# The input side of twelve pairs of steps of a GRU, computed beside the first steps, and other chunk sizes

## The chip, the cores and the metric

The kernel runs on one core of a Trainium2 chip. Its engines work side by side, each in the order of its own program: TensorE (PE; PEld is its loading of weights), VectorE (DVE), ScalarE (ACT), GpSimd (POOL) and SyncE (SP, which here issues DMA transfers). The metric is the device time of one execution in microseconds, as the median of several runs. A profile is one execution of its own.

## The reference

A GRU with 16 sequences (B), 256 steps (T) and 512 features (D) runs over x, from the state `cond_2048`. Its states go through a layer of 8 experts of rank 128, of which each token takes the two likeliest, and the result is added to x.

```python
def cell(h, x):
    gi = x @ W_ih + b_ih
    gh = h @ W_hh + b_hh
    i_r, i_z, i_n = jnp.split(gi, 3, axis=-1)
    h_r, h_z, h_n = jnp.split(gh, 3, axis=-1)
    r = jax.nn.sigmoid(i_r + h_r)
    z = jax.nn.sigmoid(i_z + h_z)
    n = jnp.tanh(i_n + r * h_n)
    h_new = (1.0 - z) * n + z * h
    return (h_new, h_new)
...
router_logits = x / norm @ router_w
routing_weights = jax.nn.softmax(router_logits.astype(jnp.float32), axis=-1)
rw, selected_experts = jax.lax.top_k(routing_weights, TOP_K)
rw = rw / jnp.sum(rw, axis=-1, keepdims=True)
...
for e in range(N_EXPERTS):
    out = out + combine[:, e, None] * (x @ Wa[e] @ Wb[e])
...
x = x + _L0_ffn_ref(_L0_cond_ref(cond_2048, x, ...), ...)
```

All of it is in 32-bit floats.

## The kernel before

**The recurrence.** The 256 steps are 32 blocks of 8 (`TS`), and 128 pairs `m` of two steps. The gates of a step stand in two PSUM banks, `rn` (r, the hidden part of n, the input part of n) and `z`; there are two sets of banks, one for even pairs and one for odd. For a pair, `seed` (L250) copies the biases into its banks with ScalarE, `trans_x` (L260) turns a tile of x with VectorE, and `gate_in` (L268) adds the input's product with `W_ih` on PE, a quarter `q` of the features at a time: 4 matmuls into `rn` (L273) and 4 into `z` (L281). Each 32-bit matmul stands as two records in the profile. The two quarters of one step belong to the next pair. `step` (L826) adds the state's product with `W_hh` (L837, L847), and then ScalarE and VectorE compute r (L863), z (L868), n (L870 to L872) and the new state (L875 to L879), which is turned into `hist` (L882) for the next step's matmuls. `back` (L887) turns it back as `h` (L890).

**The experts.** The first 29 blocks go a sparse way, in four chunks of `CHUNKS` blocks. After a block, its `Route` writes the states to DRAM (L520, eight transfers), computes the router's logits (L345) and the top two. After a chunk, a `Chunk` ranks the tokens (L372, L377), reads the states back (L468, tiles `ht2`) and scatters them by expert into slots in DRAM (L474, issued by GpSimd). A `Slab` is 128 slots of one expert: its rows are loaded (L575), GpSimd copies the expert's weights (L593, L597), VectorE turns the rows (L603), PE multiplies down (L614) and up (L629), ScalarE copies the result (L621, L637), and SP stores it (L638). A `Combine` gathers both results of each token (L666), loads x (L662), adds (L680) and stores a block of the output (L684). The last three blocks, 29 to 31, take a dense way, `Moe`: all experts (L749, L770, L786), with stores at L797.

**The planner.** The order of all this work around the steps is made in Python, when the program is built. Each agent (`Route`, `Chunk`, `Slab`, `Combine`, `Moe`) has a plan of pieces; a piece has a cost in microseconds of PE, the least number of steps since the piece before (`gap`), PE's work, what the other engines do then, and which rooms it takes and gives (`ROOM`, counts of buffers). In every step `choose` (L967) goes through the agents by rank and picks pieces. A slab's or a dense block's piece may be picked up to 0.5 us in a step, and beyond it where a running `credit`, fed from the work left and the steps left to its due time, allows. The PE part stands behind the step's own matmuls and `gate_in`, the rest behind `back`. After the last step the loop goes on until no agent is left; what it picks then makes up the tail. `keep_order` (L33) fixes the order on each engine as it was written out.

Before the first step stand the loads of all weights, in SP's queue. `clear` (L209) puts zeros into the slots, one transfer a step from step 6 on. `load_x` (L122) brings x for the block after next, in the fourth step of a block.

Of the kernel before, what the change touches and what calls it, by code (L numbers as in the profile page):

```python
# [20 lines left out]

P = 128
TS = 8
CHUNKS = [6, 10, 8, 5]
LAG = 10

ROOM = {
    "ps": 3, "xg": 4, "wg": 4, "xt": 2, "at": 2, "yg": 2, "xr": 3, "a": 1, "aT": 1,
    "hc": 2, "load": 2, "copy": 1, "turn": 2,
}  # L30


# [10 lines left out]
def gru_moe_kernel(  # L43
# [10 lines left out]
    wb: bass.AP,  # L54
    out: bass.AP,
):

# [184 lines left out]


    xts = {}

    seeds = []

    def seed(m):  # L250

        if m < T // 2:
            for n, b in enumerate((bias[:, 0:3, :], bias[:, 3:4, :])):
                b = b.rearrange("p g d -> p (g d)")
                ins = act.copy(banks[m % 2][n][:, 0 : b.shape[1]], b).ins
                if seeds:
                    tc.add_manual_dep(ins, seeds[-1].name, SYNC, reason="seen")
                seeds.append(ins)

    def trans_x(m):  # L260
        if m < T // 2:
            xt = xtp.tile([P, NQ, 32], FP, tag="xT", name=f"xT_{m}")
            dve.transpose(
                xt.rearrange("p q c -> p (q c)"), xs[m // NM][:, m % NM, :]
            )
            xts[m] = xt

    def gate_in(m, q, seen=None):  # L268

        w = wih[:, q, :].rearrange("p (g j d) -> p g j d", g=3, j=NJ)  # L270
        rn, zb = banks[m % 2]
        for j in range(NJ):
            pe.matmul(  # L273
                rn[32 * j : 32 * j + 32, 0 : 3 * P].rearrange(
                    "p (g d) -> p g d", g=3
                )[:, 0:3:2, :],
                lhsT=xts[m][:, q, :], rhs=w[:, 0:3:2, j, :],
                start=False, stop=(q == NQ - 1), skip_group_check=True,
            )
        for j in range(NJ):  # L280
            ins = pe.matmul(  # L281
                zb[32 * j : 32 * j + 32, 0:P],
                lhsT=xts[m][:, q, :], rhs=w[:, 1, j, :],
                start=False, stop=(q == NQ - 1), skip_group_check=True,
            ).ins
            if seen is not None and j == 0:
                tc.add_manual_dep(ins, seen.name, SYNC, reason="seen")
# [53 lines left out]
    def router(h):  # L341

        for q in range(NQ):
            for c in range(NJ):
                pe.matmul(  # L345
                    rt[32 * c : 32 * c + E, 0:32].rearrange("p (b t) -> p b t", t=TS),
                    lhsT=wr_sb[:, q, :], rhs=tokens(h, q, c),
                    start=(q == 0), stop=(q == NQ - 1),
                )


    class Chunk:
# [111 lines left out]
            self.w = [whi, wlo]  # L464

        def fetch(self, k):
            ht = moe.tile([P, D], FP, tag="ht2", bufs=3, name=f"ht2_{self.c}_{k}")
            sp.dma_start(ht, self.rows[k].rearrange("b t d -> (b t) d"))  # L468
            self.ht = getattr(self, "ht", {})
            self.ht[k] = ht  # L470
# [21 lines left out]
        def plan(self):  # L492
            k = self.k
            pieces = [
                Piece(gap=7, cost=0.9, pe=[("ranks",)],
                      then=[("places",), ("places2",)]),
                Piece(then=[("places3",)]),
                Piece(then=[("experts",)]),
                Piece(then=[("weights",)]),
            ] + [Piece() for _ in range(k - 2)]  # L500
            pieces[0].then[:0] = [("fetch", m) for m in range(3)]
            for m in range(k):
                pieces[2 + m].then.append(("scatter", m))
                if m + 3 < k:
                    pieces[2 + m].then.append(("fetch", m + 3))
            return pieces

    class Route:
# [185 lines left out]
    class Moe:  # L694
# [3 lines left out]

        def prep(self):
            i = self.i  # L700
            self.hc = moe.tile([P, NQ, P], FP, tag="hc", name=f"hc_{i}")
            for q in range(NQ):
                pool.tensor_copy(
                    self.hc[:, q, :].rearrange("p (b t) -> p b t", t=TS),
                    self.hist[:, :, q, 16:32].rearrange("p t b -> p b t"),
                )
            self.sq = moe.tile([P, NQ, P], FP, tag="a", bufs=1, name=f"sq_{i}")
            pool.tensor_mul(self.sq, self.hc, self.hc)
# [220 lines left out]
    def at_step(n, make):  # L929
        starts.setdefault(n, []).append(make)  # L930
# [12 lines left out]
    def slabs(c):  # L943
        ch = chunks[c]
        by = ready[c + 1] + 5 if c + 1 < len(CHUNKS) else T + 2
        ch.left = n_slabs[c]
        for n in range(n_slabs[c]):
            begin(Slab(ch, n), 1 + c, by)
# [9 lines left out]
    for c, k in enumerate(CHUNKS):  # L958
        at_step(ends[c] - k * TS, lambda c=c, k=k: chunks.append(Chunk(c, k)))
        at_step(ready[c], lambda c=c: slabs(c))  # L960
    for n in range(2):
        for k in range(n_slots[n]):
            at_step(6 + k + n * n_slots[0], lambda n=n, k=k: clear(n, k))

    credit = 0.0

    def choose():  # L967

        nonlocal credit
        rates = {}  # L970
        for a in agents:
            if a.by is not None:
                rates[a.by] = rates.get(a.by, 0.0) + sum(p.cost for p in a.todo)
        credit += sum(r / max(1, by - now) for by, r in rates.items())
        credit = min(credit, 1.3) if now <= T else 3.5
        spent = 0.0
        picked = []
        stuck = set()
        for a in agents:
            gap = now - a.since  # L980
            while a.todo and a.todo[0].gap <= gap:
                p = a.todo[0]
                key = (a.place, len(a.todo)) if a.place else None
                if key in stuck or any(room[x] < 1 for x in p.takes):
                    break
                if p.cost and a.by is not None:
                    if spent + p.cost > 0.5 and credit < 0.5 * p.cost:
                        break
                    credit -= p.cost
                spent += p.cost  # L990
                for x in p.takes:
                    room[x] -= 1
                picked.append((a, p))
                a.todo.pop(0)
                a.since = now
                gap = 0
            if a.todo and a.place:
                stuck.add((a.place, len(a.todo)))
        return picked
# [25 lines left out]
    for i in range(NB):  # L1025
        rows, rows_next = rows_next, None
        for t in range(TS):
# [8 lines left out]
            elif m + 1 < T // 2:  # L1036
                q = 0 if t % 2 == 0 else 2
                gate_in(m + 1, q)
                gate_in(m + 1, q + 1, seen)
            picked = choose()  # L1040
            advance(0, picked)
            hrow = back(hT, f"h_{i}_{t}")
            advance(1, picked)
# [16 lines left out]
    while agents or starts:  # L1060
        for make in starts.pop(now, []):
            make()
        now += 1
        picked = choose()
        advance(0, picked)
        advance(1, picked)
    keep_order(tc)
# [42 lines left out]
```

## Time and profile before

| | |
|---|---|
| median of three runs | 1322.7 us (1321.27 to 1323.1) |
| the profiled execution | 1321.0 us on the device, span 1319.1 us |
| PE busy | 1255.1 us, 95% of the span |
| VectorE, ScalarE, GpSimd busy | 742.3, 385.0, 269.0 us |
| chain that ended last, by engine | PE 82%, DVE 8%, DMA 5% |
| r (L863), first and last | 37.5 and 1224.1 us |

The page of the profile gives the busy time of each engine, and the costliest groups: L837 with 491.9 us, L273 with 318.7, L847 with 270.1, L281 with 208.5. Matmuls are pipelined, so these overlap, and their sum is no time. A granted clock of 1.0 stands in all slices but the first and the last. In the order of time a line has its start and length in us, the engine, the line of the kernel, the operation, what it writes from what it reads, and in brackets how long the engine was idle before it and what ended that. SPq is SP issuing a transfer, not the transfer itself.

### The profile page before, as it was taken

How to read it: one execution, taken by the hardware profiler on the slowest of the kernel's cores; microseconds unless marked ns; L12 is line 12 of the kernel's file. 1: busy time of each engine (PE TensorE's matmuls, PEld its weight loads, DVE VectorE, ACT ScalarE, POOL GpSimd, SP SyncE). 2: the span in 40 equal slices, each digit the busy share in tenths (PEclk: the TensorE clock that was granted, in tenths of full speed). 3: DMA queues.
4: the chain of work that ended last, by engine and by line, in shares of the span. 5: the costliest groups of instructions: out<-in, count | busy, mean ns of one | idle time of the engine just before them, and what ended most of it. 6: DMA issues, size and time to landing. Idle time of an engine off the chain costs nothing.

```text
span 1319.1 us, 68240 instructions
## 1 busy us (share of the span) xinstructions
PE 1255.1 (95%) x30378; PEld 892.0 (68%) x30378; DVE 742.3 (56%) x2678; ACT 385.0 (29%) x1330; POOL 269.0 (20%) x465
## 2 busy tenths in 40 slices
PE   6899999999999999999999999999999999999993
PEld 3566666666777777777766777777776777777551
DVE  1455555565655555555655766555655656765543
ACT  1222222222323233332332333333233333332220
POOL 2000000021100000000332321111332323543633
PEclk7999999999999999999999999999999999999997
DMA  8622222243221111111444453222543555643786
GB/s 195 178 90 91 90 68 74 87 145 96 67 59 51 46 58 43 59 55 40 162 148 123 140 154 89 71 70 71 162 148 102 148 154 160 195 158 104 220 249 182
DMA packets 142948, 151.58 MB, mean 115 GB/s; under 512 B 20726, under 2 KB 100150, under 8 KB 142652
## 3 DMA queue, kind: packets, MB, share of 16 engines
q1 hardware_dynamic: 133232, 116.74, 30.0%
q0 software_dynamic: 9280, 30.42, 7.3%
q8 instruction: 238, 3.90, 1.2%
q14 instruction: 58, 0.48, 0.1%
q10 hardware_dynamic: 140, 0.05, 0.0%
HBM read 80.28 MB, written 66.85 MB: 112 GB/s over the span
## 4 chain that ended last, share of the span: by engine, by line
PE 82%; DVE 8%; DMA 5%; ACT 2%; SPq 1%; issue 1%; DVEq 0%; ACTq 0%
PE rn L837 35%; PE z L847 17%; PE rn L273 12%; PE z L281 6%; PE at_ps L614 5%; PE y_ps L629 5%; DVE hist L882 2%; DVE zh L875 2%; DVE rows L879 2%; ACT z L868 2%; DVE m L877 2%; DMA whh<-in_L_cond_W_hh_dram 1%; PE rt L345 1%; PE o_ps L786 1%; DMA xg<-x_slots 1%
## 5 line engine op out<-in xcount | busy, mean ns | idle before, releaser
L837 PE MATMUL rn<-whh,hist 128*32 128x256 f32 x8160 | 491.9, 381 | 27.5 <-DVE hist L882 27.2
L837 PEld LDWEIGHTS rn<-whh,hist 128*32 128x32 f32 x8160 | 250.0, 110 | 202.3 <-DVE hist L882 61.4
L273 PE MATMUL rn<-wih,xT 128*32 128x256 f32 x4096 | 318.7, 382 | 8.5 <-DMA wih<-in_L_cond_W_ih_dram 7.2
L870 DVE SCALAR_TENSOR_TENSOR n<-r,rn 128x128 f32<-128x128 f32 x256 | 73.7, 288 | 368.8 <-ACT r L863 368.5
L847 PE MATMUL z<-whh,hist 128*32 128x128 f32 x8160 | 270.1, 273 | 0.0
L847 PEld LDWEIGHTS z<-whh,hist 128*32 128x32 f32 x8160 | 234.5, 110 | 42.8
L281 PE MATMUL z<-wih,xT 128*32 128x128 f32 x4096 | 208.5, 274 | 0.0
L863 ACT ACTIVATE r<-rn 128x128 f32<-128x128 f32 x256 | 71.1, 278 | 433.8 <-PE rn L837 433.6
L281 PEld LDWEIGHTS z<-wih,xT 128*32 128x32 f32 x4096 | 136.2, 111 | 87.7 <-issue 2.4
L273 PEld LDWEIGHTS rn<-wih,xT 128*32 128x32 f32 x4096 | 124.1, 111 | 9.9 <-issue 5.7
L545 POOL TENSOR_TENSOR nrm<-ss,half 128x1 f32<-128x1 f32 x29 | 16.2, 558 | 525.3 <-ACT ht L543 505.1
L875 DVE SCALAR_TENSOR_TENSOR zh<-z,h 128x128 f32<-128x128 f32 x255 | 79.8, 313 | 66.1 <-ACT z L868 65.7
L868 ACT ACTIVATE z<-z 128x128 f32<-128x128 f32 x256 | 71.1, 278 | 151.7 <-PE z L847 151.7
L614 PE MATMUL at_ps<-xgT,wag 128*32 128x128 f32 x2752 | 97.4, 273 | 3.1 <-DVE xgT L603 3.0
L629 PE MATMUL y_ps<-wbg,at 128*32 128x256 f32 x1376 | 95.1, 380 | 0.6 <-ACT at L621 0.6
L637 ACT COPY y<-y_ps 128x512 f32<-128x512 f32 x86 | 50.3, 584 | 125.5 <-PE y_ps L629 109.0
L614 PEld LDWEIGHTS at_ps<-xgT,wag 128*32 128x32 f32 x2752 | 78.8, 110 | 10.9 <-issue 4.4
L882 DVE STREAM_TRANSPOSE hist<-rows 128x128 f32<-128x128 f32 x256 | 79.7, 311 | 8.7
L890 DVE STREAM_TRANSPOSE h<-hist 128x128 f32<-128x128 f32 x256 | 79.7, 311 | 8.7
L879 DVE SCALAR_TENSOR_TENSOR rows<-zh,m 128x128 f32<-128x128 f32 x256 | 76.0, 297 | 8.9
L877 DVE SCALAR_TENSOR_TENSOR m<-z,n 128x128 f32<-128x128 f32 x256 | 79.8, 312 | 0.7 <-ACT n L872 0.7
L597 POOL COPY wbg<-wb_sb 128x512 f32 x86 | 57.7, 671 | 108.4 <-PE y_ps L629 108.3
(124 smaller groups left out, 959.2 us busy)
## 6 DMA issues: line engine op xcount, KB each, us to landing
xg<-x_slots SPq DMA_DIRECT2D x344, 64.0 KB
y_slots<-y SPq DMA_DIRECT2D x86, 256.0 KB
ht<-H SPq DMA_DIRECT2D x58, 256.0 KB
x_slots<-zero SPq DMA_DIRECT2D x50, 256.0 KB
x<-in_x_dram SPq DMA_DIRECT2D x256, 32.0 KB
xr<-in_x_dram SPq DMA_DIRECT2D x32, 256.0 KB
out_dram<-xr SPq DMA_DIRECT2D x32, 256.0 KB
H<-rows SPq DMA_DIRECT2D x232, 32.0 KB
```

Of the source, the lines that this page charges most:

```text
L273: pe.matmul(rn[32 * j : 32 * j + 32, 0 : 3 * P].rearrange("p (g d) -> p g d", g=3)[:, 0:3:2, :], lhsT=xts[m][:, q, :], rhs=w[:, 0:3:2, j, ...
L281: ins = pe.matmul(zb[32 * j : 32 * j + 32, 0:P], lhsT=xts[m][:, q, :], rhs=w[:, 1, j, :], start=False, stop=(q == NQ - 1), skip_group_chec ...
L614: pe.matmul(self.ps[c32, 0:P], lhsT=self.wa[:, q, c32], rhs=self.xt[:, q, :], start=(q == 0), stop=(q == NQ - 1),)
L629: pe.matmul(self.ps[c32, half], lhsT=self.at[:, c32], rhs=self.wb[:, half], start=True, stop=True,)
L837: pe.matmul(rn[32 * j : 32 * j + 32, 0 : 2 * P].rearrange("p (g d) -> p g d", g=2), lhsT=hT[:, q, :], rhs=w(q, j)[:, 0:3:2, :], start=Fals ...
L847: pe.matmul(zb[32 * j : 32 * j + 32, 0:P], lhsT=hT[:, q, :], rhs=w(q, j)[:, 1, :], start=False, stop=(q == NQ - 1), skip_group_check=True,)
L868: seen = act.activation(z, zb[:, 0:P], AF.Tanh, scale=0.5).ins
L875: dve.scalar_tensor_tensor(zh, z, 1.0, hrow, ALU.add, ALU.mult)
L877: dve.scalar_tensor_tensor(m, z, 1.0, n, ALU.subtract, ALU.mult)
L879: dve.scalar_tensor_tensor(hn, zh, 0.5, m, ALU.mult, ALU.subtract)
L882: dve.transpose(hist[:, t, :, lo : lo + 32], hn.rearrange("p (q c) -> p q c", q=NQ))
L890: dve.transpose(hrow.rearrange("p (q c) -> p q c", q=NQ), hT)
```

## The change

Twelve pairs, every fourth from 82 to 126, get their input side another way. An agent `Early` of rank 20 loads the pair's two steps of x with eight transfers, turns them with VectorE, multiplies them with `W_ih` into a PSUM tile of its own, copies it out with ScalarE, lets GpSimd add the biases, and stores the result in DRAM. Sixteen steps before the pair, `back` reads it into a tile `gl`, and `seed` copies that, and not the biases, into the pair's banks. `trans_x` and `gate_in` do nothing for these pairs. In the two steps in which `gate_in` for such a pair would stand, `choose` gets 1.8 us in place of 0.5, and after the last step 0. An `Early` piece is picked only within that bound. The tiles of `Early` share buffers with those of `Slab` and `Combine` (tags `yg0`, `yg1`, `at`). `hc` of the dense blocks has one buffer in place of two, `ht2` two in place of three. The chunks are of 7, 11, 7 and 4 blocks, where they were 6, 10, 8 and 5; the slabs are 21, 29, 21 and 15, where they were 19, 27, 23 and 17: 86 both times.

```diff
-CHUNKS = [6, 10, 8, 5]
+CHUNKS = [7, 11, 7, 4]
+EARLY = list(range(82, 128, 4))
-    "hc": 2, "load": 2, "copy": 1, "turn": 2,
+    "hc": 1, "load": 2, "copy": 1, "turn": 2, "early": 2,
...
     def seed(m):
         if m < T // 2:
-            for n, b in enumerate((bias[:, 0:3, :], bias[:, 3:4, :])):
+            src = early.pop(m) if m in EARLY else bias
+            for n, b in enumerate((src[:, 0:3, :], src[:, 3:4, :])):
...
     def trans_x(m):
-        if m < T // 2:
+        if m < T // 2 and m not in EARLY:
...
     def gate_in(m, q, seen=None):
+        if m in EARLY:
+            return
...
+    class Early:
+        def load(self):
+            m = self.m
+            self.x = slb.tile([P, D], FP, tag="yg1", bufs=2, name=f"xe_{m}")
+            for j in range(NJ):
+                for s in range(2):
+                    p0 = 32 * j + 16 * s
+                    sp.dma_start(
+                        self.x[p0 : p0 + B, 0:P],
+                        x[:, 2 * m + s, j * P : (j + 1) * P],
+                    )
+        def turn(self):
+            self.xt = slb.tile([P, NQ, 32], FP, tag="at", bufs=2, name=f"xTe_{self.m}")
+            dve.transpose(self.xt.rearrange("p q c -> p (q c)"), self.x[:, 0:P])
+        def into(self, what, q):
+            if what == "rn" and q == 0:
+                self.ps = big(f"gi_{self.m}").rearrange("p (g d) -> p g d", g=4)
+            w = wih[:, q, :].rearrange("p (g j d) -> p g j d", g=3, j=NJ)
+            for j in range(NJ):
+                g = self.ps[32 * j : 32 * j + 32]
+                if what == "rn":
+                    pe.matmul(
+                        g[:, 0:3:2, :], lhsT=self.xt[:, q, :], rhs=w[:, 0:3:2, j, :],
+                        start=(q == 0), stop=(q == NQ - 1),
+                    )
+                else:
+                    pe.matmul(
+                        g[:, 3, :], lhsT=self.xt[:, q, :], rhs=w[:, 1, j, :],
+                        start=(q == 0), stop=(q == NQ - 1),
+                    )
+        def keep(self):
+            gi = slb.tile([P, 4, P], FP, tag="yg0", bufs=2, name=f"ge_{self.m}")
+            act.copy(gi[:, 0, :], self.ps[:, 0, :])
+            act.copy(gi[:, 2:4, :], self.ps[:, 2:4, :])
+            pool.tensor_copy(gi[:, 1, :], bias[:, 1, :])
+            pool.tensor_add(gi[:, 0, :], gi[:, 0, :], bias[:, 0, :])
+            pool.tensor_add(gi[:, 2:4, :], gi[:, 2:4, :], bias[:, 2:4, :])
+            self.gi = gi
+        def store(self):
+            self.dram = dramc.tile([P, 4, P], FP, name=f"gd_{self.m}")
+            sp.dma_start(self.dram, self.gi)
+            at_step(2 * self.m - 16, self.back)
+        def back(self):
+            early[self.m] = moe.tile([P, 4, P], FP, tag="gl", name=f"gl_{self.m}")
+            sp.dma_start(early[self.m], self.dram)
+        def plan(self):
+            pieces = [
+                Piece(then=[("load",)], takes="early"),
+                Piece(gap=2, then=[("turn",)], takes="at"),
+            ] + [
+                Piece(gap=0, cost=c, pe=[("into", what, q)])
+                for what, c in (("rn", 0.43), ("z", 0.22))
+                for q in range(NQ)
+            ] + [Piece(then=[("store",)], gives="early")]
+            pieces[2].gap, pieces[2].takes = 1, ["ps"]
+            pieces[9].then, pieces[9].gives = [("keep",)], ["ps", "at"]
+            return pieces
...
-            ht = moe.tile([P, D], FP, tag="ht2", bufs=3, name=f"ht2_{self.c}_{k}")
+            ht = moe.tile([P, D], FP, tag="ht2", bufs=2, name=f"ht2_{self.c}_{k}")
...
-            pieces[0].then[:0] = [("fetch", m) for m in range(3)]
+            pieces[0].then[:0] = [("fetch", m) for m in range(2)]
             for m in range(k):
                 pieces[2 + m].then.append(("scatter", m))
-                if m + 3 < k:
-                    pieces[2 + m].then.append(("fetch", m + 3))
+                if m + 2 < k:
+                    pieces[2 + m].then.append(("fetch", m + 2))
...
-            self.hc = moe.tile([P, NQ, P], FP, tag="hc", name=f"hc_{i}")
+            self.hc = moe.tile([P, NQ, P], FP, tag="hc", bufs=1, name=f"hc_{i}")
...
+    at_step(2, lambda: [begin(Early(m), 20) for m in EARLY])
...
-    def choose():
+    def choose(spare):
...
-                    if spent + p.cost > 0.5 and credit < 0.5 * p.cost:
+                    if spent + p.cost > spare and credit < 0.5 * p.cost:
                         break
                     credit -= p.cost
+                if isinstance(a, Early) and spent + p.cost > spare:
+                    break
...
-            picked = choose()
+            picked = choose(1.8 if m + 1 in EARLY else 0.5)
...
-        picked = choose()
+        picked = choose(0.0)
```

More of the change, by code (lines that the diff above doesn't have):

```diff
@@ L246, in gru_moe_kernel @@
     xts = {}
+    early = {}
     seeds = []
@@ L349, in router, with __init__ @@
                 )
+    class Early:
+        def __init__(self, m):
+            self.m = m
+        def load(self):
[54 more added lines that the diff above has]
+            return pieces
```

## The prediction

> **What bounds the kernel now.** I looked first at busy time by stretches of 50 us, because one core that is 95% busy on average can still be bound by two different things. The columns are the stretch, then for PE, PEld, DVE, ACT and POOL the busy us with the count of instructions, then clock, DMA share and GB/s.
>
> ```profile
> 200.00:250.00 50.00, 47.03 (x1143) 32.71 (x1138) 27.00 (x111) 13.77 (x52) 1.08 (x6) 1.00 0.20 64
> 400.00:450.00 50.00, 50.00 (x1256) 35.79 (x1249) 27.93 (x109) 16.27 (x59) 3.78 (x9) 1.00 0.17 48
> 1100.00:1150.00 50.00, 50.00 (x1280) 38.16 (x1272) 33.85 (x115) 16.52 (x55) 18.46 (x26) 1.00 0.60 176
> ```
>
> PE seems full from 400 us on, yet that says nothing of pace: the starts of r (L863) are 4.40 us apart at 200 us and also at 400 us, and about 5.2 us apart at 1100 us. So I went to the order of time on PE within a step, first at 200 us (start, length, line):
>
> ```profile
> 201.65 0.61 PE L273 MATMUL rn<-wih,xT 128*32 128x256 f32 x8
> 202.08 0.40 PE L281 MATMUL z<-wih,xT 128*32 128x128 f32 x8
> 202.78 0.42 PE L837 MATMUL rn<-whh,hist 128*32 128x256 f32 x4 [0.30 <-DVE hist L882]
> ```
>
> The input side of one quarter takes 0.43 us of issue for r and n (201.65 to 202.08) and 0.22 for z, so 0.65, and 1.30 us in a step. After it PE waits for the new state. By issue the hole is 202.78 - 202.30 = 0.48 us. At 400 us one slab piece of 0.43 us fills it and the step stays at 4.40. The step is then bound by the loop of the recurrence: 1.9 us of L837, the two tanh, five VectorE operations. Late, the hole is overfilled:
>
> ```profile
> 1104.84 1.05 PE L629 MATMUL y_ps<-wbg,at 128*32 128x256 f32 x16
> 1105.70 0.63 PE L614 MATMUL at_ps<-xgT,wag 128*32 128x128 f32 x16
> 1106.14 1.92 PE L837 MATMUL rn<-whh,hist 128*32 128x256 f32 x32
> ```
>
> Three pieces (1.29 us by issue) lie between 1104.84 and 1106.14 and L837 has no wait any more: PE sets the end. From the starts of r, grouped by the pieces that stand in the built order of PE, the medians are 4.40 us with 0 or 1 piece, 4.77 with 2, 5.20 with 3, 5.63 with 4. This gives the rule I sum by: **step = the larger of 4.405 and 3.91 + X**, with X the extra PE work (3.91 = 4.77 - 0.86). Over steps 2 to 255 it gives 1170.3 us; measured are 1182.3. The 12.0 us between are ranks, late transfers and the collision shown below.
>
> After the last step (its r at 1224.12) come 95 us of tail: PE works until 1298.4, and then 20.7 us pass on SP's queue alone:
>
> ```profile
> 1299.17 0.58 SPq L797 DMA_DIRECT2D out_dram<-xr  x1
> 1299.83 0.56 SPq L684 DMA_DIRECT2D out_dram<-xr  x1
> 1300.48 2.15 SPq L662 DMA_DIRECT2D xr<-in_x_dram  x2
> 1305.69 3.18 SPq L684 DMA_DIRECT2D out_dram<-xr  x2
> 1308.96 0.59 SPq L662 DMA_DIRECT2D xr<-in_x_dram  x1
> 1314.50 0.55 SPq L684 DMA_DIRECT2D out_dram<-xr  x1
> ```
>
> Block 31's store (L797) waits for the last matmul. Behind it in SP's order stand three loads of xr, with their adds and stores.
>
> **The change, part by part.** 1. *Late steps.* In 24 steps (the two before each of the 12 pairs, steps 163 and 164 to 251 and 252) 1.30 us of L273 and L281 are gone, so there the rule is 2.61 + X, and the planner may put 1.8 us there. 24 x 1.30 = 31.2 us are moved. I put the built PE order of both programs through the rule, step by step. Before: 46 steps with two pieces lose 0.37 each (16.8), 25 with three lose 0.79 (19.9), 19 others, mostly with a route, 14.8: 51.5 us over the floor. After: 23 lose 0.37 (8.4), 19 lose 0.79 (15.1), 14 others 12.3: 35.8 us. **-15.7 us**. Not all 31 come back. Chunk 1's slabs may begin 17 steps later (step 165, not 148), so about a dozen steps there that carried two or three pieces now carry one. Two of the freed steps fill partly with the last pair's own pieces, and steps 221 and 222 stand empty.
>
> 2. *Early steps.* 11 pairs run in steps 6 to 85, the twelfth at 163 to 169. A step takes either 0.43 or 0.44 us, which fits 0.48: no price on PE, as at 400 us. Without this cover (where ranks fall together with a piece) it would be 0.4 us each. ACT gets two copies per pair (0.27 as L621 has, about 0.38 between L255's 0.27 and 0.49), before the seed; the seed ends 2.4 us before the next r in the timeline, so they fit.
>
> 3. *The turn on VectorE.* 12 more transposes (0.28, L263's row) stand behind h (L890) in the order; from there to the next n VectorE has some 2.4 us free. What queues behind a late turn is n (L870), and with it the whole loop. Each waits for 8 loads issued two steps (8.8 us) earlier. SP needs 3.6 to 4.8 us for eight loads of x, 8.8 to 9.7 us for eight stores of H. The worst case is a load placed right behind the stores (step 41): 1.7 + 9.7 + 4.2 us of issue and about 2.2 to land make 17.8 after step 40's r; the cover ends at 17.9. The first two pairs queue 16 loads behind the 2 MB of wb_sb, which hold SP to 1.07 us per load until 55.5 us; landing 58 to 62 against a cover to 59.7. I take +2, from 0 to +6.
> [...] The rows above, with eight in flight and two steps of cover, give +2.
>
> 4. *GpSimd's adds.* 36 operations (0.43 as L703; adds between 0.43 and 1.03 by L703 and L708). The trace has such a meeting:
>
> ```profile
> 311.93 0.72 POOL L597 COPY wbg<-wb_sb 128x512 f32 x1
> 312.09 0.70 DVE L877 SCALAR_TENSOR_TENSOR m<-z,n 128x128 f32<-128x128 f32 x1
> ```
>
> L877 takes 0.28 elsewhere, and this step took 4.82, 0.42 more. 36 meetings would be 15 us; but beside 172 copies of weights only 15 of 254 steps exceed the rule by over 0.15 us with no rank in them. I take +1.5, from 0 to +5.
> [...]
>
> 5. *ht2 with two buffers, not three.* A block's scatter holds GpSimd 2.3 us, and landing plus refetch some 5 more (one fetch shows 4.09 in the chain of waits), so two buffers give a block every 3.7 us against a step of 4.4. POOL's own waits for ht total 6.2 us now. +2, from 0 to +6.
> The 12 stores and 12 reloads (0.4 us of SP each) have 13 steps until the seed that needs them; I take nothing; a reload that misses its seed would stop ACT, and r behind it, for its landing, 2 to 4 us.
>
> 6. *Tail.* Until block 30's last matmul PE has 51.4 us of work now and takes 57.2 from the last r; after, 50.7 us, but the 13 slabs left stand denser (3.4 us each, not 4.1), against SP's 2.0 us of xg loads, y store and combine per slab. I take 59.3, **+2**, from -2 to +8. With hc single, block 31 starts behind block 30: route, 64 matmuls (7.08), two turns, 64 matmuls (7.07), as now 17.1 less one y piece (0.86): 16.3 us. Its xr waits for the second combine's store, lands some 18.1 later; add 0.7, three adds more 2.3, last store 4.6 to the end: 25.7 us after block 30's end. Now it is 1319.1 - 1281.3 = 37.8, since three loads queue behind L797; in the new order none does, and the last chunk has four blocks. **-12**, from -14 to -3.
>
> **Sum** against the profiled span: -15.7 + 2 + 1.5 + 2 + 2 - 12 = -20.2, so 1319.1 to 1298.9. That run took 1321.0 on the device, 1.7 under the median of the three (1322.7); 1322.7 - 20.2 is about **1302 us**.
>
> **The rivals.** *A: filled on paper only.* PE's order is known, its waits are not. In a freed step an "up" needs ACT's copy and a y buffer of two; in the tail ACT's y copies waited 16.5 us for y stores. If the dense steps and slabs lose a third of the two gains: +9, about 1311. Against it: only 5 us of the tail's 57 are PE waits today.
> *B: the turns come late, and it ends slower.* Place: L378's transposes on VectorE, ahead of n. Price: each us by which the eight loads miss the cover stretches 12 steps. From 1.7 us on average (20.2 / 12) the gain is gone; at 2.5 us it is 1332. For it: step 41's sum leaves 0.1 us. Against it: most loads lie between SP's bursts, with over 5 us to spare.
> *C: the work isn't moved.* The built order has no L273 row for these pairs, and 12 x 8 early ones; excluded.
> *D: the 12 us outside the rule shrink too*, as fewer dense steps collide: 1292.
>
> **How the numbers follow.** Forecast 0.60, A 0.24, B 0.10, D 0.06. The forecast's own range is 1294 to 1309; A's lower part and D widen it to **1291 to 1316**, which leaves B and A's tail out, 2 in 10. This kernel's runs spread 0.14%, so 0.2% (2.6 us) is what tells a change from none. Slower: B, 0.10. Same: 0.03, from A and B where they just cancel. Faster: 0.87.
>
> **What would show it.** Steps before 48 still 4.40 apart (part 2), a step near 60 us longer by 0 to 3 (3); freed steps at 4.40 with four pieces (1); r of the last step at about 1213 (1 to 5); no load of xr behind block 31's store, and some 10 us from the last matmul to the end (6). Waits of VectorE on xe of over 20 us, or freed steps near 5 us, would make it wrong.

## The result, and the profile after

The changed kernel takes 1306.8 us, the median of four runs (1301.67 to 1308.58), against 1322.1 us beside it. The ratio is 0.988, with a 95% interval of 0.985 to 0.991. The prediction was 1302, from 1291 to 1316. The profiled execution is the fastest of the four: 1301.67 us, with a span of 1299.9 (predicted: 1298.9). So the sum was 1 us from the one run that can be read in the trace, and 5 us from the median. The starts of r divide the difference of the two profiled spans:

| us | before | after | difference | predicted |
|---|---|---|---|---|
| start to first r | 37.5 | 37.3 | -0.2 | 0 |
| first r to last r | 1186.6 | 1179.6 | -7.0 | -10.2 |
| last r to block 30's last matmul | 57.2 | 56.6 | -0.6 | +2 |
| from there to the end | 37.8 | 26.4 | -11.4 | -12 |
| span | 1319.1 | 1299.9 | -19.2 | -20.2 |

First the busy time by the same stretches as before (columns as there):

```profile
200.00:250.00 50.00, 50.00 (x1244) 35.54 (x1236) 27.59 (x116) 14.14 (x54) 3.73 (x10) 1.00 0.28 94
400.00:450.00 50.00, 50.00 (x1288) 36.65 (x1284) 26.92 (x103) 16.17 (x58) 5.23 (x12) 1.00 0.23 67
1100.00:1150.00 50.00, 48.74 (x1240) 36.35 (x1229) 36.24 (x118) 17.76 (x57) 22.84 (x32) 1.00 0.66 193
```

At 200 us PE was 47.03 of 50 us busy; now it is full, with 101 records more, and r still comes every 4.40 us. The order of time on PE shows what fills it, and then what a late freed step looks like:

```profile
202.67 0.61 PE L281 MATMUL rn<-wih,xT 128*32 128x256 f32 x8
203.10 0.40 PE L289 MATMUL z<-wih,xT 128*32 128x128 f32 x8
203.31 0.61 PE L387 MATMUL gi<-wih,xTe 128*32 128x256 f32 x8
203.79 0.42 PE L914 MATMUL rn<-whh,hist 128*32 128x256 f32 x4
...
1197.28 1.08 PE L924 MATMUL z<-whh,hist 128*32 128x128 f32 x32
1198.15 1.07 PE L706 MATMUL y_ps<-wbg,at 128*32 128x256 f32 x16
1199.01 1.08 PE L691 MATMUL at_ps<-xgT,wag 128*32 128x128 f32 x32
1199.95 1.93 PE L914 MATMUL rn<-whh,hist 128*32 128x256 f32 x32
```

An early piece (L387) lies where PE waited 0.48 us for the state. In the freed step no L281 and no L289 stand between L924 and L914; four pieces take their place (1198.15 to 1199.95), and r follows after 4.40 us, where four pieces beside the input side took 5.63 before.

The largest loss stands at the start. These lines of the timeline are SP's and VectorE's around the first early pairs:

```profile
46.87 0.45 SPq L178 DMA_DIRECT2D wb_sb<-in_L_ffn_Wb_dram  x1
47.36 14.24 SPq L371 DMA_DIRECT2D xe<-in_x_dram  x16
...
58.23 0.31 DVE L378 STREAM_TRANSPOSE xTe<-xe 128x128 f32<-128x128 f32 x1 [0.75 <-DMA xe<-in_x_dram]
63.12 0.31 DVE L378 STREAM_TRANSPOSE xTe<-xe 128x128 f32<-128x128 f32 x1 [4.58 <-DMA xe<-in_x_dram]
63.36 0.27 DVE L269 STREAM_TRANSPOSE xT<-x 128x128 f32<-128x128 f32 x1
63.55 0.25 DVE L947 SCALAR_TENSOR_TENSOR n<-r,rn 128x128 f32<-128x128 f32 x1
```

The second pair's turn waits 4.58 us for its loads, and n (L947), which the loop needs, stands behind it. This step takes 9.39 us and the next 5.02. A second long step, of 7.31 us, stands at 767.7 (SP's rows, then ScalarE's):

```profile
753.15 4.04 SPq L545 DMA_DIRECT2D ht<-H  x2
757.28 0.38 SPq L715 DMA_DIRECT2D y_slots<-y  x1
762.08 0.32 SPq L545 DMA_DIRECT2D ht<-H  x1
762.50 6.05 SPq L597 DMA_DIRECT2D H<-rows  x8
770.40 0.33 SPq L605 DMA_DIRECT2D ht<-H  x1
...
773.17 0.63 ACT L620 ACTIVATE ht<-ht 128x512 f32<-128x512 f32 x1 [4.14 <-DMA ht<-H]
...
773.80 0.56 ACT L714 COPY y<-y_ps 128x512 f32<-128x512 f32 x1
774.26 0.48 ACT L261 COPY rn<-bias 128x384 f32<-128x384 f32 x1
...
774.99 0.27 ACT L940 ACTIVATE r<-rn 128x128 f32<-128x128 f32 x1
```

SP stands still from 757.7 to 762.1 before it can issue a fetch into ht2 (L545). Eight stores of H and the router's own read of H (L605) are queued behind that fetch. ScalarE then waits 4.14 us for the read, with the seed (L261) and r (L940) behind it. The summed waits for H, on GpSimd's scatters (L551) and on ScalarE (columns: engine, line, what ended it; us in total, times, longest), say how often:

```profile
POOL x_slots L551 <- DMA ht<-H: 49.8, 16, 6.9
...
ACT ht L620 <- DMA ht<-H: 6.4, 4, 4.1
```

Before, GpSimd's waits for ht were 6.2 us. The end of SP's queue:

```profile
1288.17 0.54 SPq L790 DMA_DIRECT2D xr<-in_x_dram  x1
1293.25 0.59 SPq L874 DMA_DIRECT2D out_dram<-xr  x1
1293.91 1.99 SPq L761 DMA_DIRECT2D out_dram<-xr  x2
```

No load of xr stands behind block 31's store (L874). The last matmul ends at 1289.8, 10.1 us before the end, where it was 20.7.

### The profile page after: what moved, and what is told of

The parts are those of the page before. It is cut to its first block, busy times and chain, and to the rows that moved or that the text cites. A ratio compares the mean times of both kernels' runs of the same rounds, so it can differ in the third digit from the quotient of the medians.

```text
span 1299.9 us, 68450 instructions
## 1 busy us (share of the span) xinstructions
PE 1252.2 (96%) x30378; PEld 888.0 (68%) x30378; DVE 734.4 (56%) x2678; ACT 391.4 (30%) x1354; POOL 285.4 (22%) x504
## 5 line engine op out<-in xcount | busy, mean ns | idle before, releaser
L914 PE MATMUL rn<-whh,hist 128*32 128x256 f32 x8160 | 493.6, 382 | 19.4 <-DVE hist L959 16.5
L914 PEld LDWEIGHTS rn<-whh,hist 128*32 128x32 f32 x8160 | 247.7, 110 | 201.4 <-DVE hist L959 51.8
L281 PE MATMUL rn<-wih,xT 128*32 128x256 f32 x3712 | 287.9, 381 | 11.3 <-DMA wih<-in_L_cond_W_ih_dram 9.4
L947 DVE SCALAR_TENSOR_TENSOR n<-r,rn 128x128 f32<-128x128 f32 x256 | 73.2, 286 | 362.2 <-ACT r L940 361.2
L924 PE MATMUL z<-whh,hist 128*32 128x128 f32 x8160 | 271.0, 273 | 0.0
L924 PEld LDWEIGHTS z<-whh,hist 128*32 128x32 f32 x8160 | 235.5, 110 | 42.9 <-issue 0.4
L940 ACT ACTIVATE r<-rn 128x128 f32<-128x128 f32 x256 | 70.9, 277 | 426.4 <-PE rn L914 426.4
L289 PE MATMUL z<-wih,xT 128*32 128x128 f32 x3712 | 188.4, 274 | 0.0
L289 PEld LDWEIGHTS z<-wih,xT 128*32 128x32 f32 x3712 | 122.0, 111 | 80.4 <-issue 1.8
L281 PEld LDWEIGHTS rn<-wih,xT 128*32 128x32 f32 x3712 | 112.0, 110 | 12.9 <-DMA wih<-in_L_cond_W_ih_dram 5.1
L952 DVE SCALAR_TENSOR_TENSOR zh<-z,h 128x128 f32<-128x128 f32 x255 | 77.7, 305 | 65.6 <-ACT z L945 65.4
L706 PE MATMUL y_ps<-wbg,at 128*32 128x256 f32 x1376 | 94.6, 380 | 0.8 <-ACT at L698 0.8
L949 ACT ACTIVATE n<-n 128x128 f32<-128x128 f32 x256 | 77.3, 302 | 7.6 <-DVE n L948 7.3
```

Of the source, the lines that this page charges most:

```text
L281: pe.matmul(rn[32 * j : 32 * j + 32, 0 : 3 * P].rearrange("p (g d) -> p g d", g=3)[:, 0:3:2, :], lhsT=xts[m][:, q, :], rhs=w[:, 0:3:2, j, ...
L289: ins = pe.matmul(zb[32 * j : 32 * j + 32, 0:P], lhsT=xts[m][:, q, :], rhs=w[:, 1, j, :], start=False, stop=(q == NQ - 1), skip_group_chec ...
L706: pe.matmul(self.ps[c32, half], lhsT=self.at[:, c32], rhs=self.wb[:, half], start=True, stop=True,)
L914: pe.matmul(rn[32 * j : 32 * j + 32, 0 : 2 * P].rearrange("p (g d) -> p g d", g=2), lhsT=hT[:, q, :], rhs=w(q, j)[:, 0:3:2, :], start=Fals ...
L924: pe.matmul(zb[32 * j : 32 * j + 32, 0:P], lhsT=hT[:, q, :], rhs=w(q, j)[:, 1, :], start=False, stop=(q == NQ - 1), skip_group_check=True,)
L947: dve.scalar_tensor_tensor(n, r, 1.0, rn[:, P : 2 * P], ALU.add, ALU.mult)
```

## The experiments

They ran in three groups. In the first, the kernel before took 1322.1 us; in the second and third the same kernel took 1404.5 and 1405.9, and all others were longer too (the last section shows where that time lies). Times are therefore compared within a group and by their ratio to the kernel before. The changed kernel itself ran in none of the later groups.

**First group. The old chunk sizes.**

```diff
-CHUNKS = [7, 11, 7, 4]
+CHUNKS = [6, 10, 8, 5]
```

> The changed kernel with the old chunk sizes (6, 10, 8, 5), early pairs, single hc and two ht2 kept. Theory: the tail's gain comes from the chunk sizes, because only they bring the combines of the last chunk ahead of block 31 in SP's order; in this kernel's built order three loads of xr stand behind block 31's store again. Then the steps gain what the rule gives (1152.7 us against 1154.6 in the changed kernel, so -1.9), the stretch from the last matmul to the end is about 20 us and not 10, and the time is 1306.8 - 1.9 + 11 = about 1316 us (1312 to 1320). Rival: the single hc buffer makes the tail short; then the tail stays at about 83 us from the last r and the time is about 1305 us.

1316.8 us, ratio 0.996 (0.995 to 0.998), as the first theory had it. The last r is at 1217.6, the tail 96.1 us, and 20.7 us lie after the last matmul. With early pairs and a single hc, but old chunks, the short tail is gone.

**The chunk sizes alone.**

```diff
-EARLY = list(range(82, 128, 4))
+EARLY = []
```

> The changed kernel without any early pair; chunk sizes, single hc, two ht2 and the planner's bound of 0 in the tail kept. Theory: the tail keeps its 83 us from the last r (-12 against before), no stall near 59 us, steps before 48 at 4.40 throughout, and the rule gives 1171.8 us for the steps (before: 1170.3), so 1322.1 - 12 + 1.5 + 0 to 3 for late ht = 1312 to 1315 us. The early pairs are then worth 5 to 8 us net, not the 17 of the rule (1171.8 - 1154.6), since the stall near 59 us (5.6) and other late transfers take the rest. Rival: the chunk sizes alone bring nothing and it ends near 1322; or they bring all of it, near 1307.

1320.4 us, ratio 0.999 (0.998 to 1.000), dearer than the theory. In time the first rival, 1322, is nearer and the interval reaches 1; yet the tail did get shorter, so it isn't that the chunk sizes bring nothing. Last r at 1229.0, 4.9 us later than before (the rule gave 1.5), tail 86.5 and not 83. It also holds a long step at the same place, 8.07 us in the 164th, without any early pair. By this kernel as a control, the early pairs cost nothing on the steps that they run beside: steps 12 to 48 take 158.57 us here and 158.64 with them, steps 48 to 64 70.69 and 70.71, steps 64 to 100 160.73 and 161.70, where the rule accounts for 1.0. From r to r the early pairs are worth 12.2 us net. With the stall at the start (5.6) put back it is 17.8, and the rule's own difference was 17.2.

The two halves alone give 5.3 us (old chunks) and 1.8 us (chunks alone), together 15.3: they don't add. Their tails, 96.1 and 86.5 beside 95.0 before and 83.0 with both, show that the chunk sizes alone bring 8.5 of the 12.0 us; the early pairs bring nothing there with the old chunks and 3.5 with the new ones.

**Early pairs begin later.**

```diff
-    at_step(2, lambda: [begin(Early(m), 20) for m in EARLY])
+    at_step(6, lambda: [begin(Early(m), 20) for m in EARLY])
```

> The early pairs begin at step 6, not 2; all else as in the changed kernel. Theory: the step of 9.39 us at 59.2 us and the next of 5.02 are long because the first sixteen loads of xe stand behind wb_sb on SP (14.24 us for 16) and the turn on VectorE waits for them with the loop behind it. From step 6 they are issued after wb_sb has gone, so no step before 48 is over 4.8 us, the first 48 steps take about 207 and not 212.7, the rule adds 1.2 us elsewhere, and the time is 1306.8 - 5.6 + 1.2 = about 1302 us (1300 to 1304). Rival: eight loads of 8 KB take longer than two steps wherever they are issued; then a step of 7 to 9 us stands some 20 us later and the time stays at 1306 to 1308.

1304.1 us, ratio 0.987 (0.985 to 0.989). The stall is gone and has not moved elsewhere: steps 1 to 12 take 48.45 us, not 54.06, and the sixth 4.41. SP's line is now

```profile
57.10 9.35 SPq L371 DMA_DIRECT2D xe<-in_x_dram  x16
```

for the same sixteen loads, 9.35 us and not 14.24, now that wb_sb is no longer ahead of them. The median fell by only 2.7, and the profiled span by 1.2. In the profile, 1.2 us come back as PE's other order (steps 100 to 147; the rule gives 1.9) and 2.2 in steps 147 to 170, where the 164th takes 8.51 us.

**Three ht2 buffers.**

```diff
-            ht = moe.tile([P, D], FP, tag="ht2", bufs=2, name=f"ht2_{self.c}_{k}")
+            ht = moe.tile([P, D], FP, tag="ht2", bufs=3, name=f"ht2_{self.c}_{k}")
...
-            early[self.m] = moe.tile([P, 4, P], FP, tag="gl", name=f"gl_{self.m}")
+            early[self.m] = moe.tile([P, 4, P], FP, tag="gl", bufs=1, name=f"gl_{self.m}")
```

> ht2 has three buffers again and three fetches go ahead; to make room, gl has one buffer and the reload of an early pair comes 9 steps before its use, not 16. Theory: the step of 7.31 us at 767.7 us and the 49.8 us that GpSimd's scatters wait for ht come from the two buffers; with three, GpSimd's wait falls to some 6 us, no step from 147 to 170 is over 6 us, and the time is some 3 us less, about 1303.5 us (1302 to 1306). Rival: GpSimd's wait falls but nothing on the loop waited for it, and the late ht at 767.7 us was SP's queue; then the step stays and the time is the same to 1 us. A single gl that comes too late would show as ScalarE waiting for gl ahead of its seed.

1302.0 us, ratio 0.985 (0.983 to 0.987); five runs spread from 1300.5 to 1304.3. The 164th step takes 4.41 us, and the waits for H are

```profile
POOL x_slots L551 <- DMA ht<-H: 4.1, 3, 2.3
...
ACT ht L620 <- DMA ht<-H: 3.5, 2, 2.2
```

So the two buffers were the cause of the long step, and the single gl shows no wait. The gain in time is less sure: the medians differ by 4.8 us, but the profiled spans by 0.1 (1299.9 and 1299.8), since steps 147 to 170 are 2.3 us shorter, and steps 1 to 12 are 0.9 and steps 170 to 255 are 1.6 longer. The stall at the start is still there (10.09 us in the sixth step).

**Second group. Both mended, and block 31's own x buffer.**

> The early pairs begin at step 6 and ht2 has three buffers (gl one). Theory: the two stalls are independent. The stall near 59 us took 6.5 us in the run with three ht2 alone, and beginning later costs 1.2 us by the rule; the stall near 768 us (3 to 4 us) is gone with three ht2. The medians of the two runs, 2.7 and 4.8 us under the changed kernel's 1306.8, then add up: about 1299 us, by the stretches of the profile nearer to 1297 (range 1296 to 1301). Steps before 48 all within 0.1 us of 4.40, GpSimd's wait for ht under 8 us. Rival: what one stall gives back is taken by the next late transfer; then about 1302, as with either part alone.

1378.3 us beside 1404.5, ratio 0.982 (0.980 to 0.983). The profile answers for the stalls: the first 48 steps take the rule's time to 0.1 us, and no wait for ht is left among those listed. Whether the two gains add up in time can't be read from this group: steps 64 to 100 took 175.5 us and steps 147 to 170 130.6, by the stretches that the last section shows.

```diff
-            self.xr = moe.tile([P, D], FP, tag="xr", bufs=3, name=f"xr_{i}")
+            self.xr = moe.tile([P, D], FP, tag="ht2" if i == 31 else "xr", bufs=3, name=f"xr_{i}")
...
-            sp.dma_start(out[:, i * TS : (i + 1) * TS, :], self.xr)
+            q = act if i == 31 else sp
+            q.dma_start(out[:, i * TS : (i + 1) * TS, :], self.xr)
```

> As the kernel with both mended stalls, and block 31's x goes into a buffer of ht2, which nobody uses by then, and not into one of the three xr buffers, and its store is issued by ScalarE's queue. Theory: in the tail, block 31's final add on VectorE waits 1.7 us for an xr that could not be loaded before a combine's store had read its buffer, and the two last stores stand behind block 31's on SP; both go, and the stretch from the last matmul to the end falls from 10.1 to about 8 us: 1 to 3 us under the kernel with both mended stalls. Rival: the last combine, not block 31, sets the end; then no change.

1376.3 us, ratio 0.981 (0.979 to 0.982), not told apart from the one without. The stretch after the last matmul stays at 9.9 us. The own buffer hardly brings x sooner. Its load goes out some 2 us earlier against the end, right behind two loads of combines, but takes 6.30 us to land, where it was 4.21 in the kernel with both mended: VectorE waits 1.31 us for it (1.69 in the changed kernel). The rival held in that nothing changed and the last combine's store ends last. But in the chain that ended last, that combine's adds stand behind block 31's add on VectorE, and this behind its x, so the two can't be told apart.

**Block 31's store last, in the kernel before** (the lines for its own x buffer and for the single hc are not shown).

```diff
         def store(self):
+            if self.i == 31:
+                last.append(self.finish)
+            else:
+                self.finish()
+
+        def finish(self):
             i = self.i
             dve.tensor_add(self.xr, self.ps.pop("o"), self.xr)
...
+    for f in last:
+        f()
     keep_order(tc)
```

> The kernel before with old chunks and without early pairs; only block 31's last add and store are issued after all combines, with an x buffer of its own (room from a single hc, which leaves the built order of PE and SP as it was). Theory: the tail's gain is one of queue order. With the store out of the way the two loads of xr behind it go out as soon as the combine ahead has stored, at about 1297.5 and not 1300.5; the last load then goes at about 1303.5 and not 1309, and its store some 7 us earlier: 1322.1 - 7 = about 1315 us (1312 to 1317), with every step as before. Rival: what shortens the tail is that the last chunk has four blocks and fewer slabs; then nothing changes here, 1321 to 1323.

1399.3 us, ratio 0.997 (0.996 to 0.998), so 5 us less, but not where the theory put it: 20.1 us still lie after the last matmul and the tail is 95.4. SP's queue shows why:

```profile
1373.74 4.18 SPq L685 DMA_DIRECT2D out_dram<-xr  x2
1377.97 1.27 SPq L663 DMA_DIRECT2D xr<-in_x_dram  x2
1384.67 2.03 SPq L685 DMA_DIRECT2D out_dram<-xr  x2
1386.80 0.59 SPq L663 DMA_DIRECT2D xr<-in_x_dram  x1
1393.42 0.55 SPq L685 DMA_DIRECT2D out_dram<-xr  x1
1394.02 0.59 SPq L804 DMA_DIRECT2D out_dram<-xr  x1
```

Block 31's store (L804) is out of the way, and the loads still come in rounds: two loads, two adds and stores, one load, one store. Five combines pass through three xr buffers, and the rounds take their time by themselves. The store in the queue is not what makes these rounds. Where the 5 us came from is open, since the kernel before has no profile in this group. They need not lie in the steps: a kernel with the same steps, in the third group (slabs first), has its last r at 1304.1 us, and this one at 1303.4. So it isn't shown that the store had no part in the tail.

**Two hc buffers again** (gl one buffer, as above, and `ROOM` with two for `hc`).

```diff
-            self.hc = moe.tile([P, NQ, P], FP, tag="hc", bufs=1, name=f"hc_{i}")
+            self.hc = moe.tile([P, NQ, P], FP, tag="hc", bufs=2, name=f"hc_{i}")
```

> The changed kernel with two hc buffers again (gl one buffer, reload 9 steps ahead). Theory: the chunk sizes bring the short tail, and the single hc does nothing for it: the built order of the last block is the same as in the changed kernel, the rule differs by 0.2 us, and the time is 1305 to 1308 us with some 10 us after the last matmul. Rival, as the prediction put it: the single hc holds block 31 behind block 30 and so lets the combines go first; with two the tail is longer by 5 us or more, 1312 or above.

1369.7 us, ratio 0.976 (0.975 to 0.977): in its group the best. No long tail came back: it is 86.8 us, beside 84.7 of the kernel with both mended stalls, with 12.2 us after the last matmul and 34.1 from the last y to the end. The single hc is not what shortens the tail. That this kernel is 8.6 us under the one with both mended stalls was not foreseen. It differs from it in the begin, in ht2 and in hc at once; its 159th step takes 8.21 us where that one's takes 16.04, both with PE idle in the way that the last section shows; summed over PE and its weight loads, this idle time is 122 us here and 138 there. No run separates these.

**Two terms of the tail.** The kernels up to here, put beside each other by the end of the last L706 (the last y of a slab), suggest two terms:

| kernel | y's left at the last r | last r to last y | last y to end |
|---|---|---|---|
| before | 16 | 59.0 | 36.1 |
| changed | 13 | 49.2 | 33.8 |
| old chunks | 16 | 60.1 | 36.0 |
| chunks alone | 15 | 51.2 | 35.3 |
| begin later | 13 | 49.5 | 33.9 |
| three ht2 | 13 | 49.1 | 33.5 |
| both mended | 13 | 49.6 | 35.1 |
| both mended, own x buffer | 13 | 49.3 | 35.1 |
| store last (before) | 16 | 59.4 | 36.0 |
| two hc | 13 | 52.7 | 34.1 |

The y's left are counted in the built order of PE. By division each takes 3.4 to 4.1 us, the dense work between them included, and from the last one to the end it is 33.5 to 36.1. With 15 left the last y comes nearly as soon as with 13, so their number isn't all. The third group tried both terms.

**Third group. Four blocks last, with a late last slab.**

```diff
-CHUNKS = [7, 11, 7, 4]
+CHUNKS = [6, 10, 9, 4]
```

> The changed kernel with chunks of 6, 10, 9 and 4 blocks: the last chunk has four blocks and 15 slabs as in the changed kernel, but the planner puts its last slab behind block 30's work, into block 31's. Theory: the end comes 34 to 36 us after the last slab's y, whatever PE does after it (in every run so far it did, from 33.5 to 36.1). By the rule the steps take 9.4 us less, and PE's work in the order puts the last y at about 69 us from the last r and the last matmul some 13 us later; so the end is about 104 us from the last r, the span about 1207.5 + 104 = 1311 us and the time 1313 to 1317, with some 21 us after the last matmul. Rival: four blocks in the last chunk make the short tail, with 10 us after the last matmul; then 1302 to 1307.

1389.4 us beside 1405.9, ratio 0.988 (0.985 to 0.990). The tail is 116.1 us, the longest of all: last y after 76.5 us (18.5 left, 4.1 each), 39.6 to the end, 26.8 after the last matmul. The rival is out: a last chunk of four blocks makes no short tail. The theory's end, 104, was too low by 12, of which 7.5 lie before the last y and 4.6 behind; so the 34 to 36 us are no rule. Its steps were the shortest of the group (last r at 1271.8, against 1292.8 for both mended).

**Slabs first**, in the kernel before and in the one with both mended stalls.

```diff
+        held = now > T and any(isinstance(a, Slab) for a in agents)
         for a in agents:
+            if held and isinstance(a, Moe) and a.i >= 30:
+                continue
             gap = now - a.since
```

> The kernel before with one line more in the planner: after the last step, blocks 30 and 31 wait until no slab is left. Chunks, buffers and all steps stay as they were. Theory: the tail is set by when the last y is there. PE's work ahead of it falls from 52 to about 36 us by issue, so the last y comes some 43 and not 59 us after the last r; behind it stand 32 us of dense work, so the combines are hidden and PE ends last: last matmul at about 78, end at 86 to 88 us from the last r and not 95. Time 1322.1 - 8 = about 1314 us (1311 to 1318). Rival: slabs alone can't go faster than SP brings their loads, and PE's idle time takes the gain back: 1320 or more.

> The kernel with both mended stalls and the same line in the planner. Theory: here the combines are nearly hidden already; the last y moves from 49 to about 40 us from the last r, and PE with its last store sets the end at 80 to 82 us and not 83 to 84.7: 2 us (0 to 4) under the kernel with both mended stalls. Rival: the denser slabs wait for SP and it ends 0 to 5 us above.

Slower, both of them, than without it: 1409.5 us, ratio 1.002 (1.001 to 1.004), and 1383.0, ratio 0.984 (0.981 to 0.986), against 0.979 (0.977 to 0.982) of the kernel with both mended, run once more beside them (its runs end at 1380.4 us, where those of slabs first begin at 1380.5). With block 30's work gone from ahead of it, the last y comes 58.0 us after the last r (59.0 in the kernel before's only profile, of an earlier group), and in the other kernel 47.3, not 50.8. In the kernel before with slabs first PE now waits 14.1 us for ScalarE's copies (0.6 in the kernel before). These are waits of several engines from the last r to the last y:

```profile
ACT y L637 <- PE y_ps L629: 19.4, 11, 3.2
...
PE y_ps L629 <- ACT at L621: 14.1, 9, 6.1
DVE xr L680 <- DMA xg<-x_slots: 9.2, 2, 6.2
ACT y L637 <- DMA y_slots<-y: 8.8, 2, 7.3
```

With 16 and 13 y's left that is 3.6 us each, and taking dense work out from between them hardly helps. Yet 3.6 us is no pace of the slabs themselves: in the same trace some y's start 2.47 us after one another. The longest hold is this one (rows of SP, ScalarE and PE):

```profile
1341.57 0.59 SPq L662 DMA_DIRECT2D xr<-in_x_dram  x1
1342.26 0.54 SPq L638 DMA_DIRECT2D y_slots<-y  x1
...
1347.20 0.59 ACT L637 COPY y<-y_ps 128x512 f32<-128x512 f32 x1 [7.27 <-DMA y_slots<-y]
...
1348.10 2.24 PE L629 MATMUL y_ps<-wbg,at 128*32 128x256 f32 x16 [6.08 <-ACT at L621]
```

SP waits 3.7 us, until 1341.57, to load x for a combine (L662), because a store out of xr has not ended. A y store is queued behind that load. ScalarE's next copy of y waits 7.27 us for a y store, and PE 6.08 us for ScalarE. This makes 6.1 of PE's 14.1 us; the other eight waits are not followed here. The dense work must then be done behind the slabs: 44.6 and 43.5 us from the last y to the end, so the second term doesn't hold here either.

**Both mended, once more.**

> The kernel with both mended stalls (begin at step 6, three ht2) once more, since in its group PE got its instructions late for stretches of several us, in all kernels alike, and the kernel before took 1404.5 us. Without that: 1299 us (1296 to 1301), as expected then, no step of over 5 us before 300 us and steps from 147 to 170 within 2 us of the rule's 101.9. With it: a ratio to the kernel before of about 0.982 again.

1378.5 us, ratio 0.979 (0.977 to 0.982): the second case of the expectation. Against the changed kernel's 0.988, taken in another group, this is no proof that it is the better one. What is shown is that the long steps go. In time, either mend alone gave 0.987 and 0.985 in the first group, each with an interval that overlaps the changed kernel's.

Not tried: the early pairs without GpSimd's adds, and a slab's chain with more buffers.

## Why the prediction was right

*1, late steps (-15.7)*: right. Of the 24 freed steps 22 take 4.40 to 4.54 us, with up to four pieces; the others are 4.75 and the 7.31 shown above.

*2, early steps (0)*: right, by the control without early pairs: 0.07 us over 36 steps.

*3, the turn (+2, 0 to +6)*: the place was right, the first two pairs behind wb_sb, and the size was at the upper end: 5.6 us. The step that was mis-sized is "landing 58 to 62 against a cover to 59.7": the second turn ran at 63.1, and the loads issued 16 in 14.2 us. All later pairs came in time: before their turns VectorE waits 0.56 us at most. Rival B, that the turns come late on average, has no other case in the trace.

*4, GpSimd's adds (+1.5)*: nothing to be seen; steps 12 to 64, in which the results of seven pairs get their biases, are 0.1 us over the control. The 15 us of 36 meetings like the one at 311.93 did not come. In the trace an operation of VectorE on the loop overlaps an add eleven times, and each of the eleven takes 0.29 us, its usual length. Nine of them are n's two operations (L947, L948); the two zh (L952) overlap by only 0.05 and 0.13 us. None is m, the operation that took 0.70 us beside a copy of weights at 311.93, so what an add would cost it is not shown.

*5, two ht2 (+2, 0 to +6)*: steps 147 to 170 are 5.5 us over the rule, where they were 2.0 before, and three buffers took 2.3 us off them (4.8 in the median). The working was wrong in its queue: I held "a block every 3.7 us" against the step, as if only GpSimd waited. The fetch that waits for its buffer stands on SP, and eight stores and the router's read of H stand behind it.

Parts 3 to 5 were +5.5; over the rule the changed kernel lost 8.7 more than before (20.7 against 12.0), and -15.7 + 8.7 is the -7.0 measured.

*6, tail (+2 and -12, together -10)*: measured -12.0. The sum held and the mechanism didn't, so that it held is in part luck. I wrote that the end is short "since three loads queue behind L797" and the single hc puts block 31 behind block 30. The single hc is in the kernel with the old chunks, whose tail is long (96.1), and not in the one with two hc, whose tail is short (86.8); moving the store alone left 95.4. The traces show in their place that the last y comes 9.8 us sooner after the last r, and the end 2.3 us sooner after it. Ahead of the last y PE is idle for 3.6 us before and 3.0 after, so PE's work sets most of it. In the changed kernel this holds 13 y's and not 16 (48 records fewer each of y_ps and at_ps, by the prediction's issue times 3.9 us), and only one dense block's second multiplication (o_ps, L786) and not two (64 records fewer of 128; 7.1 us by the prediction's figure), since block 30's now follows the last y. Of the first multiplication (a_ps, L749) 12 records more stand there (1.3 us), which leaves 9.7. The chunk sizes alone move that multiplication back (68 records, 15 y's, last y after 51.2 us); only with the early pairs as well are 13 y's left. No run takes away the planner's bound of 0 after the last step; with the old chunks it made no short tail.

Rival A, dense steps filled on paper only, is out by the freed steps; by the median alone it wouldn't be, since 1306.8 is as near to its 1311 as to 1302. Rival D, that fewer dense steps collide, is out too: from step 170 on, 7.2 us over the rule before and 6.6 after. The 5 us between the profiled run and the median of the changed kernel have no profile and stay open.

## What to carry to other kernels

In this kernel a fetch that waited for its buffer held up all that SP had queued behind it (for 4.4 us, to 762.1, with eight stores and a read behind it): when a buffer is taken away, ask what else that queue issues in the time, not only whether the consumer keeps pace. Look for what the tail hangs on by lining up several kernels at candidate events, and then test the event in kernels built to break it: from the last y to the end it was 33.5 to 36.1 us in ten kernels, and 39.6 to 44.6 in the three that were built as a test. What helps then is to count the work and the idle time that PE has ahead of the event. Work put into PE's idle time was free here only from the moment that its operands could be there: begun in the burst of the start it cost the first steps 5.6 us, begun behind it nothing, so such loads belong behind the burst, not in it.

## What the hardware showed unexpected

In the later groups PE stood idle for stretches of several us in which the trace names nothing that it waited for, at the same steps each time that the same steps ran (the 66th, 153rd and 159th in all four runs with both stalls mended). The expectations call this late instructions; that is a reading and not shown. The busy time from 326 to 334 us, first of the kernel with both mended stalls (second group), then of the changed kernel (columns as above):

```profile
326.00:334.00 8.00, 4.93 (x23) 1.30 (x21) 0.28 (x1) 0.15 (x1) 4.90 (x5) 0.79 0.78 242
```

```profile
326.00:334.00 8.00, 8.00 (x217) 5.70 (x211) 5.42 (x23) 1.94 (x8) 3.99 (x5) 1.00 0.57 193
```

PE has 23 records where it had 217, while GpSimd's scatters and SP's stores ran on. Summed over PE and its weight loads, idle time of this kind ("issue") is 44 to 49 us in every kernel of the first group, in the kernel before and in the changed one, and 115 to 159 in the eight of the later groups. Within the steps most of it lies where GpSimd issues scatters: between the sixth and the last r of the kernel with both mended stalls it is 97 us, 68 of them in the 21 steps with scatters (3.9 in the changed kernel, 0.8 in its 29 such steps). That is a place and not yet a cause, since the first group has the same scatters. A change of chip isn't the cause, because the first two groups ran on the same one; nor is the clock, granted at 0.980 to 0.991 on average in the later groups and 0.985 to 0.992 in the first, where the time differs by 6%. The kernel's instructions have a DMA queue of their own, with packets, MB and share of the DMA engines' time in the page of the kernel with both mended stalls:

```profile
q8 instruction: 238, 3.90, 1.2%
```

3.90 MB in 238 packets is 16.4 KB each. That PE ran dry because one of them came late is the author's guess. They took no more of the DMA engines' time than in the changed kernel (238 packets, 1.3% there), and no run here shows that one was late, nor why PE stands idle only in the later groups.
